# Experts' first layer: from seven products on two-by-two chunks to fifteen on three-by-three-by-two chunks

## The chip, the cores and the metric

The kernel runs on one core of one Trainium2 chip. The metric is the device time of one launch in microseconds (us), the median of several runs. The engines are named as in the profile: PE (TensorE, matrix products, with PEld for its loading of weights), DVE (VectorE), ACT (ScalarE), POOL (GpSimd) and SP (SyncE, which issues most DMAs). Products accumulate in PSUM, in banks of 512 float32 columns; everything else lives in SBUF.

## The reference, cut to what matters

Two layers run over 4 x 1024 tokens of 384 channels. Layer 0 is a deformable attention, layer 1 a linear attention followed by a mixture of experts. The change touches only the experts:

```python
probs = softmax(t @ gate_w + gate_b)              # 4 experts, the best 2 of each token are kept
h = gelu(einsum('bsd,edh->ebsh', t, w1) + b1)     # first layer: 384 -> 1536 units, float32
y = einsum('ebsh,ehd->ebsd', h, w2) + b2          # second layer: 1536 -> 384
out = einsum('bse,ebsd->bsd', masked_probs, y)
```

## The kernel before, in words

The experts run after everything else has nearly ended, from about 1626 us of the span on. The tokens of each expert are cut into 25 blocks: 13 of 512 tokens, 3 of 256 and 9 of 128 (`PHASES`, L40). `ORDER` (L43) fixes their sequence. Written by sizes, with S for 128, it is 512, 512, 512, S, 512, S, 256, 512, S, 512, S, 256, 512, S, 512, S, 256, 512, S, 512, S, 512, S, 512, 512. So six blocks of 512 follow an S, three follow a 256, three follow a 512, and each 256 stands between an S and a 512.

A block's 384 inputs are three chunks of 128 (rows of the first layer's weights `w1`), its 1536 units are twelve chunks of 128. A block of 512 or 256 tokens ("long") is computed with half-blocks of m tokens (256 or 128) as columns:

- The first layer takes two unit chunks at a time (class `Pair`, L2568 on). On the first two input chunks it uses a two-by-two-by-two scheme of seven products P1 to P7 of m columns; the third input chunk is multiplied plainly (`plain`, L2589), which is four more half-width products. A pair thus costs eleven products of m columns, and a block six pairs. Each product on float32 is two PE instructions. Partial results are read out of PSUM while their bank goes on accumulating: ACT copies y after P1 and P5 (L2599), after P6 (L2613) and after P7 (L2630), and DVE adds at L2614, L2615 and L2631.
- The sums of weights that the scheme needs are made by POOL (`first_sums_steps`, L2112 on, four operations of 128x384 for each half of the units, L2121 to L2124). Likewise `second_sums` (L2508 on, four operations of 128x1152) for the second layer. The sums of tokens are made by DVE (`token_sums`, L2494 on, L2503 to L2506).
- The second layer (L2660) is seven accumulated products P1 to P7; DVE makes sums of the hidden units (L2653), adds bias (L2548) and results (L2556) to the rows of the output.
- A block of 128 (`short_block`) uses plain products (L2750, L2762) and no sums. It is called S here.

The order on each engine is written by hand (`tc.manual_schedule`): each engine does its instructions in program order. On POOL, a block j puts in its queue at its start the weight sums of its own second half of units (`first_sums(d, 1)`), `second_sums` part 0, the gather of output rows so far (`rows_so_far`, L2535), `second_sums` part 1, and the first half's sums of the next block (`first_sums(nxt, 0)`); in the middle the gather of the block after next (L2071, one indirect DMA for each 128 tokens); at the end the stores of its rows (`store_rows`, L2563). For an S block only the gathers, the stores and `first_sums(nxt, 0)` remain. For the first block both halves' sums are made long before, between 1525 and 1534 us; its own gathers, `second_sums` and the last routing table entries (L2256) stand before its hooks on POOL. Transposes of the next block (`turn`, PE L2489, DVE copy L2492) and its token sums are spread through the second layer.

Dependencies between engines (semaphores) are set by the framework from the tiles that instructions read and write. PSUM pools: `lmm` with four banks, `lph` and `ltr` with two each.

Of the kernel before, what the change touches and what calls it, by code (L numbers as in the profile page):

```python
# [284 lines left out]
def body(  # L285
# [1819 lines left out]
    HALF_V = HC // 4  # L2105
# [6 lines left out]
    def first_sums_steps(d, half):  # L2112

        if short(d):
            return
        w = d["w1"].rearrange("p a (v m j) -> p a v m j", m=2, j=P)[:, :, half * HALF_V : (half + 1) * HALF_V]
        a11, a21, a12, a22 = w[:, 0, :, 0], w[:, 0, :, 1], w[:, 1, :, 0], w[:, 1, :, 1]
        t = wsum.tile([P, 3, HALF_V, P], F32, tag=f"wa{half}", name=f"wa{half}_{d['i']}")
        s1, s2, s4 = (t[:, k] for k in range(3))
        d["A", half] = dict(P1=a11, P2=a12, P3=s4, P4=a22, P5=s1, P6=s2, P7=a21)  # L2120
        yield nc.gpsimd.tensor_tensor(s1, a21, a22, ALU.add)  # L2121
        yield nc.gpsimd.tensor_tensor(s2, s1, a11, ALU.subtract)  # L2122
        yield nc.gpsimd.tensor_tensor(s4, a12, s2, ALU.subtract)  # L2123
        yield nc.gpsimd.tensor_tensor(a21, a11, a21, ALU.subtract)  # L2124
# [4 lines left out]
    with tc.tile_pool(name="c_1", bufs=1) as c1, tc.tile_pool(name="c_2", bufs=2) as c2, tc.tile_pool(  # L2129
# [255 lines left out]
        def outputs(b):  # L2385
# [42 lines left out]
            if b == 2:  # L2428
                d = state["block"]
                gather(d, ds0, state["added"])  # L2430
                sums = (i_ for half in range(2) for i_ in first_sums_steps(d, half))
            yield
            for k in range(NB):
# [12 lines left out]
                i_ = next(sums, None)  # L2446
                if i_ is not None:
# [26 lines left out]
    with tc.tile_pool(name="d_w1", bufs=1) as dw1, tc.tile_pool(name="d_s1", bufs=1) as ds1, tc.tile_pool(  # L2474
        name="d_2", bufs=2
    ) as d2p, tc.tile_pool(name="d_h", bufs=1) as dh:
        homes = [(dw0, ds0), (dw1, ds1)]
        ds = {0: first}
# [15 lines left out]
        def token_sums(d):  # L2494
# [5 lines left out]
            b11, b12, b21, b22 = x[:, 0, :m], x[:, 0, m:n], x[:, 1, :m], x[:, 1, m:n]  # L2500
            t = d2p.tile([P, 3, 256], F32, tag="xc", name=f"xc{d['i']}")
            t1, t2, t4 = (t[:, k, :m] for k in range(3))
            nc.vector.tensor_tensor(t1, b12, b11, ALU.subtract)  # L2503
            nc.vector.tensor_tensor(t2, b22, t1, ALU.subtract)
            nc.vector.tensor_tensor(t4, b21, t2, ALU.subtract)
            nc.vector.tensor_tensor(b12, b22, b12, ALU.subtract)  # L2506
            d["B"] = dict(P1=b11, P2=b21, P3=b22, P4=t4, P5=t1, P6=t2, P7=b12)
# [66 lines left out]
        class Pair:  # L2574

            def __init__(self, d, v):
                self.d, self.v, self.m = d, v, d["size"] // 2
# [304 lines left out]
```

## Time and profile before

| what | us |
|---|---|
| median of three runs (2637.04 to 2641.66) | 2637.63 |
| the profiled execution's own time | 2639.53 |
| its span, first to last instruction | 2637.8 |
| PE / POOL / DVE / ACT busy in the span | 2476.7 / 1376.8 / 1810.1 / 1102.1 |
| experts: first product to last instruction | 1626.1 to 2637.8 |
| a 512 block after an S: first layer (2188.83 to 2220.92) | 32.09 |
| the same block: second layer (2220.92 to 2245.31) | 24.39 |
| the S block after it (2245.31 to 2261.75) | 16.44 |
| the 256 block after that: first layer, second layer | 18.70, 16.29 |

Reading: "busy" is the union of an engine's instructions, a time after "idle before" is the wait before an instruction and after the arrow stands what ended it. A float32 product appears as "x2" in the timeline, its two passes.

### The profile page before, as it was taken

What the parts mean: (1) busy time and instruction counts of PE and PEld (TensorE: products, weight loads), DVE (VectorE), ACT (ScalarE), POOL (GpSimd) and SP (SyncE); (2) the same over time, 40 slices, a digit from 0 to 9 for tenths busy, and PEclk for the clock granted to TensorE, in tenths of its full rate; (3) what the DMA queues carried; (4) which work ended last, traced back from release to release, by engine and by line L of the source; (5) the groups of instructions that cost most, each with busy time, mean ns of one, the idle gap of its engine ahead of it and who ended that gap; (6) DMA issues with size and microseconds to landing.
All of it is one profiled execution on the core that took longest, in us unless ns stands there. A gap on an engine that the chain in (4) does not pass through costs nothing. (4 is left out here: it accounts for less than half of the span.)

```text
span 2637.8 us, 39381 instructions
## 1 busy us (share of the span) xinstructions
PE 2476.7 (94%) x15017; PEld 1573.9 (60%) x15017; DVE 1810.1 (69%) x2921; ACT 1102.1 (42%) x1818; POOL 1376.8 (52%) x1132
## 2 busy tenths in 40 slices
PE   8989958889999999999999997999999999999999
PEld 5555423333333333333466654888888898888888
DVE  3888959989999999999766667444453444443443
ACT  5666525556666665665433322222222222222222
POOL 1468855765666566566113346444354544734443
PEclk9999979999999999999999998999999999999999
DMA  7774465565556555554312113435545534644431
GB/s 214 199 223 131 146 197 161 151 175 151 156 165 192 175 169 163 158 153 128 120 36 72 65 61 109 150 114 180 186 150 183 192 123 171 234 162 160 151 132 36
DMA packets 263320, 395.42 MB, mean 150 GB/s; under 512 B 134674, under 2 KB 207634, under 8 KB 262748
## 3 DMA queue, kind: packets, MB, share of 16 engines
q1 hardware_dynamic: 214912, 230.43, 28.2%
q0 software_dynamic: 47504, 162.42, 19.5%
q8 instruction: 118, 1.93, 0.3%
q14 instruction: 70, 0.57, 0.1%
q10 hardware_dynamic: 716, 0.07, 0.0%
HBM read 335.95 MB, written 70.06 MB: 154 GB/s over the span
## 5 line engine op out<-in xcount | busy, mean ns | idle before, releaser
L1443 PE MATMUL ps<-q,k 64*64 64x512 f32 (+1 forms) x1632 | 380.4, 583 | 39.9 <-DMA k<-k_d 18.4
L1448 PE MATMUL ps<-t,o 64*64 64x512 f32 (+3 forms) x1536 | 351.8, 572 | 0.0
L1324 POOL DMA_INDIRECT win<-table,widx x192 | 286.6, 1493 | 71.0 <-issue 24.9
L2563 POOL DMA_INDIRECT out<-rows,ei x67 | 67.3, 1004 | 410.9 <-DVE rows L2556 389.8
L1015 POOL DMA_INDIRECT ga<-img,pidx x168 | 205.8, 1225 | 137.9 <-DVE w L972 64.2
L1385 ACT ACTIVATE t<-win,bw 128x1056 f32<-128x1056 f32 x192 | 207.4, 1093 | 128.5 <-DVE S L1475 100.2
L1475 DVE SCALAR_TENSOR_TENSOR S<-t,bw,ps 128x1024 f32<-128x1024 f32 x192 | 237.1, 1277 | 33.8 <-PE ps L1448 31.2
L1443 PEld LDWEIGHTS ps<-q,k 64*64 64x64 f32 x1632 | 104.0, 134 | 259.7 <-issue 193.1
L1548 POOL TENSOR_TENSOR S<-S,pbs 128x896 f32<-128x896 f32 (+1 forms) x69 | 136.8, 1982 | 180.2 <-DVE t L1396 174.7
L1553 ACT ACTIVATE S<-S 128x2048 f32<-128x2048 f32 x96 | 183.4, 1911 | 97.7 <-DVE S L1540 97.7
L1567 PE MATMUL po<-S,v 128*64 128x512 f32 x768 | 193.4, 615 | 24.5 <-ACT S L1553 24.1
L1396 DVE SCALAR_TENSOR_TENSOR t<-win,bw,t 128x1056 f32<-128x1056 f32 (+3 forms) x169 | 196.2, 1196 | 14.4 <-ACT t L1385 11.3
L2660 PE MATMUL b<-w,h 128*128 128x192 f32 x1044 | 180.3, 326 | 0.0
L2660 PEld LDWEIGHTS b<-w,h 128*128 128x128 f32 x1044 | 171.3, 190 | 2.4
L1540 DVE TENSOR_TENSOR S<-S,pbs 128x2048 f32<-128x2048 f32 (+1 forms) x96 | 158.8, 1656 | 13.3 <-ACT pbs L1529 13.3
L2492 DVE COPY d_xT<-e_tr 128x512 f32<-128x512 f32 (+2 forms) x75 | 37.6, 511 | 172.4 <-PE e_tr L2489 172.4
L2599 ACT COPY snap<-y 128x256 f32<-128x256 f32 (+1 forms) x96 | 33.9, 353 | 267.8 <-PE y L2582 267.1
L2256 POOL DMA_INDIRECT tab_d<-ent,si x64 | 65.7, 1027 | 146.8 <-DVE selw L2249 126.9
L2756 ACT ACTIVATE h<-ph,b1c 128x128 f32<-128x128 f32 x108 | 30.9, 369 | 265.0 <-PE ph L2750 265.0
L2614 DVE TENSOR_TENSOR snap<-y,snap 128x256 f32<-128x256 f32 (+1 forms) x96 | 38.4, 400 | 147.6 <-ACT snap L2613 147.5
L2660 PE MATMUL b<-wb,hs 128*128 128x192 f32 x696 | 119.3, 329 | 7.5 <-DVE rows L2556 7.5
L2631 DVE TENSOR_TENSOR y<-y,third 128x256 f32<-128x256 f32 (+1 forms) x96 | 39.1, 407 | 123.0 <-ACT third L2630 123.0
(413 smaller groups left out, 5767.6 us busy)
## 6 DMA issues: line engine op xcount, KB each, us to landing
w<-in_L_ffn_w SPq DMA_DIRECT2D x50, 2304.0 KB
img<-in_x SPq DMA_DIRECT2D x48, 256.0 KB
q<-q_d SPq DMA_DIRECT2D x48, 256.0 KB
x<-in_x SPq DMA_DIRECT2D x8, 768.0 KB
q_d<-qt SPq DMA_DIRECT2D x24, 256.0 KB
v_d<-qkvw SPq DMA_DIRECT2D x32, 192.0 KB
k<-k_d SPq DMA_DIRECT2D x48, 128.0 KB
v<-v_d SPq DMA_DIRECT2D x24, 256.0 KB
```

Source lines behind the costliest of these rows:

```text
L1015: nc.gpsimd.indirect_dma_start(out=ga[:, g].rearrange("p s c -> p (s c)"), out_offset=None, in_=img[b][:, :], in_offset=bass.IndirectOffse ...
L1324: i_ = nc.gpsimd.indirect_dma_start(out=win[:, : (WROWS - free_rows(nb)) * WIN], out_offset=None, in_=tables[h // 2][:, :], in_offset=bass ...
L1385: i_ = nc.scalar.activation(t.rearrange("p y x -> p (y x)"), wins[p, e][:, :n], AF.Copy, scale=weight(p, e, 0),)
L1396: state["gate"] = nc.vector.scalar_tensor_tensor(tf, wins.pop((p, e))[:, WIN : WIN + ts[p, e].shape[1] * WIN], weight(p, e, 1), tf, ALU.mu ...
L1443: made.append(nc.tensor.matmul(ps[HALF[1 - r], e, q_at], k[HALF[r], 2 * kp + e, :], q[HALF[r], q_at], start=(step == 0), stop=(step == 1 a ...
L1448: made.append(nc.tensor.matmul(ps[HALF[r], d, at], os_[p, d][HALF[r], :], wholes[p, d][HALF[r], at.start // WI : at.stop // WI, 0:WI], sta ...
L1475: nc.vector.scalar_tensor_tensor(st[:, e, :].rearrange("p (y x) -> p y x", x=WI), wholes.pop((p, e))[:, :, 1:WIN], weight(p, e, 3), ps[:, ...
L1540: state["gate"] = nc.vector.tensor_tensor(at_, at_, bc(pbss[p // KP][:, cols_], 1, 2), ALU.add)
L1548: i_ = nc.gpsimd.tensor_tensor(at_, at_, bc(pbss[p // KP][:, c_:], 1, 2), ALU.add)
L1553: nc.scalar.activation(Ss[p], Ss[p], AF.Exp)
L1567: nc.tensor.matmul(pos[i][0][HALF[f], :], vs[i][:, 2 * kp + e, :], Ss[p][:, e, FULL[f]], start=(first and e == 0), stop=(last and e == 1),)
L2660: nc.tensor.matmul(out[:, k * NH : (k + 1) * NH], h[:, v, k * P : (k + 1) * P], w[:, v, :], start=(start and v == 0 and k == 0), stop=True ...
```

## The change

The first layer of long blocks now takes three unit chunks, all three input chunks and two token halves at a time, with a scheme of fifteen products q1 to q15 (class `Trio` in place of `Pair`), four trios to a block: 60 products of m columns where there were 66. Nothing of the second layer's arithmetic changes. Two accumulations run in turn, `alpha` (six products in the right half of bank x, for the trio ahead) and `beta` (five products in the right half of bank y); their running contents are tapped, by ACT copies in alpha and by DVE adds in beta, before the next product is added. `two` and `three` put one product each in the left halves of y and x; `shared` and `one` use a bank z of their own. The weight sums become 13 POOL operations of 128x256 for each half of the units, in place of 4 of 128x384. The token sums become 12 DVE operations and one ACT operation, in two parts. For the first block, only the first half's weight sums are still made early; the second half's are now in its `start` hook. The alpha of a block's first trio (`begin`) is issued before the block begins: between the second layer's P3 products of a long block, or the last quarter of an S block's second layer. Transposes of the next block move earlier. The core of the diff, added lines with their places:

```diff
@@ first_sums_steps
-        yield nc.gpsimd.tensor_tensor(s1, a21, a22, ALU.add)
...
+        t = (state["halves"] if half else wsum).tile([P, 6, GH, P], F32, tag=f"wa{half}", name=f"wa{half}_{d['i']}")
+        n0, n1, n2, n3, n4, n5 = (t[:, k] for k in range(6))
+        d["A", half] = dict(
+            q1=a31, q2=a11, q3=n5, q4=n2, q5=a12, q6=n3, q7=n4, q8=a13, q9=n1, q10=n0, q11=a21, q12=a23, q13=a22,
+            q14=a32, q15=a33,
+        )
+        for out_, one, other, op in (
+            (n0, a21, a33, ALU.add), (a31, a31, a32, ALU.add), (n1, a21, a31, ALU.add), (a31, a11, a31, ALU.add),
+            (n2, a32, a31, ALU.subtract), (n2, n2, a33, ALU.subtract), (n3, a13, a23, ALU.subtract),
+            (n4, a21, n3, ALU.subtract), (n3, n3, a22, ALU.add), (n5, a31, a12, ALU.add), (n5, n5, n3, ALU.subtract),
+            (a23, a23, a33, ALU.add), (a23, a23, a22, ALU.subtract),
+        ):
+            yield nc.gpsimd.tensor_tensor(out_, one, other, op)
@@ token_sums(d, part)
+            if part == 0:
+                nc.scalar.mul(x9, b11, -1.0)
+            for out_, one, other, op in (
+                (
+                    (x0_, b12, b11, ALU.subtract), (b12, b12, b22, ALU.subtract), (x1, b12, b32, ALU.subtract),
+                    (x2, b11, x1, ALU.subtract), (x3, b11, b22, ALU.subtract),
+                ),
+                (
+                    (x6, b32, b31, ALU.subtract), (x7, x6, b12, ALU.subtract), (x5, b21, b31, ALU.add),
+                    (x4, b21, b22, ALU.subtract), (b21, b11, b21, ALU.subtract), (x8, b22, b31, ALU.add),
+                    (b32, b22, b32, ALU.add),
+                ),
+            )[part]:
+                nc.vector.tensor_tensor(out_, one, other, op)
@@ class Trio
+            def alpha(self, k):
...
+                self.product(("q10", "q11", "q9", "q1", "q2", "q4")[k], self.x, self.right, start=k == 0)
+                if k < 5:
...
+                    nc.scalar.copy(to, self.x[:, self.right])
+            def beta(self, k):
...
+                self.product(("q15", "q12", "q6", "q8", "q7")[k], self.y, self.right, start=k == 0)
+                if k < 4:
...
+                    nc.vector.tensor_tensor(to, self.y[:, self.right], to, ALU.add)
+                else:
+                    nc.vector.tensor_tensor(self.y[:, self.both], self.y[:, self.both], self.th[:, self.both], ALU.add)
+            def shared(self):
+                self.z = lph.tile([P, 512], F32, tag="ph", name="z")
+                self.product("q3", self.z, self.left, start=True)
...
+            def one(self):
+                self.product("q5", self.z, self.left)
...
+            def two(self):
+                self.product("q13", self.y, self.left)
+            def three(self):
+                self.product("q14", self.x, self.left)
...
@@ long_block, first layer
+                order = (
+                    "a0 t q b0 a1 r b1 a2 s b2 a3 u p b3 a4 b4 v a5" if ahead else
+                    "f t q f b0 f r f b1 f s f b2 f u p f b3 f f b4 v"
+                ).split()
+                # a, b: alpha of the trio ahead, beta; q shared, r two, s three, p one;
+                # t, u, v: gelu of the trio before's second, this one's third and first unit chunk;
+                # f: a step of the second layer's P1
@@ long_block, second layer
             if nxt:
-                turn(nxt, 1)
+                turn(nxt, 2)
+                token_sums(nxt, 0)
             add_rows(d, high, 1, b3_)
             second_product(d, "P7", b1_, range(HV), False)
...
+            third, more = second_steps(d, "P3", b3_, range(HV), False), begin(nxt)
+            for _ in third:
+                next(third, None)
+                next(more, None)
+            for _ in more:
+                pass
             add_rows(d, high, 1, b1_)
             add_rows(d, high, 0, b1_)
             store_rows(d, high)
+            if nxt:
+                token_sums(nxt, 1)
             add_rows(d, low, 1, b3_)
@@ short_block, behind first_layer(2)
+                turn(nxt, 2)
+                token_sums(nxt, 0)
+            second_layer(0)
+            second_layer(1)
             add_bias(d, 0)
-            second_layer(2)
+            if nxt:
+                token_sums(nxt, 1)
+            second_layer(2, True)
+            for _ in more:
+                pass
@@ before the blocks
+            for part in range(2):
+                token_sums(first, part)
+            for _ in begin(first):
+                pass
@@ hooks("start")
                         if j == 0:
+                            first_sums(d, 1)
                             first_sums(nxt, 0)
```

In the written order a and b are alpha of the trio ahead and beta; q is `shared`, r `two`, s `three`, p `one`; t, u, v are the gelu of the trio before's second and of this trio's third and first unit chunk (ACT); f is a step of the second layer's P1 (one product of 192 columns, two PE instructions). In the second layer of a long block `turn(nxt, 0)` now stands behind P4, `turn(nxt, 1)` behind P6 and `turn(nxt, 2)` behind P5; in an S block `turn` of parts 0 and 1 stands before the last third of its first layer. `begin(d)` issues the six alphas of trio 0; `second_layer(2, True)` issues one of them before each of its four products.

## The prediction, as it was put on record

> **What bounds the kernel now.** I read the page's busy times, then the experts' stretch alone: the windows of single stages, the timeline of one pair, POOL's timeline, and the waits. PE is busy 94% of the span, and in the experts' 512 blocks all of the time. The windows (length; busy us of PE, PEld, DVE, ACT, POOL; clock) of a 512 block's first and second layer, the S behind it, and a 256 block's two layers:
>
> ```profile
> 2188.83:2220.92 32.09, 31.94 (x141) 25.92 (x140) 10.54 (x20) 14.15 (x29) 21.25 (x16) 1.00 0.41 132
> 2220.92:2245.31 24.39, 24.39 (x153) 24.32 (x151) 14.39 (x25) 0.69 (x1) 1.85 (x2) 1.00 0.30 106
> 2245.31:2261.75 16.44, 16.44 (x104) 13.16 (x103) 5.03 (x9) 3.43 (x12) 8.34 (x10) 1.00 0.97 330
> 2261.75:2280.45 18.70, 18.37 (x132) 15.77 (x130) 7.38 (x20) 9.53 (x29) 17.06 (x13) 1.00 0.68 228
> 2280.45:2296.74 16.29, 13.74 (x88) 13.27 (x87) 15.22 (x20) 0.47 (x1) 10.76 (x8) 1.00 0.43 159
> ```
>
> Here PE sets the end, except in the 256 block, where POOL works 17 of 18.7 us. Now the timeline inside a pair:
>
> ```profile
> 2199.56 1.02 PE L2589 MATMUL x<-d_xT,w 128*128 128x512 f32 x2
> ...
> 2203.88 0.59 PE L2582 MATMUL y<-xc,wa 128*128 128x256 f32 x2
> ...
> 2204.31 1.02 PE L2589 MATMUL x<-d_xT,w 128*128 128x512 f32 x2
> 2204.56 0.37 ACT L2599 COPY snap<-y 128x256 f32<-128x256 f32 x1 [0.49 <-PE y L2582]
> ...
> 2204.99 0.37 PEld L2582 LDWEIGHTS y<-xc,wa 128*128 128x128 f32 x2 [0.49 <-ACT snap L2599]
> 2205.16 0.59 PE L2582 MATMUL y<-xc,wa 128*128 128x256 f32 x2
> ```
>
> A pair lasts 2204.31 - 2199.56 = 4.75 us for eleven half-width products: 0.431 each, with no wait left on PE. And the tap has a length: product 0.59, then 0.09, copy 0.37, 0.05 to the weights, 0.18 to the next product in the same bank, 1.28 from start to start; it is hidden because three products' time (1.29) lies between. With DVE as the reader: 0.59, some 0.03, 0.43 (L2614), 0.15 from its end to the product (below), 1.20. **I take 1.25 for both.**
>
> ```profile
> 1897.39 0.28 DVE L2614 TENSOR_TENSOR snap<-y,snap 128x128 f32<-128x128 f32 x1
> ...
> 1897.82 0.46 PE L2582 MATMUL y<-d_xT,w 128*128 128x128 f32 x2 [0.59 <-DVE snap L2614]
> ```
>
> This product is P7: it writes the left half of y, and it waits for a DVE add that reads the right half. A bank is guarded as a whole.
>
> POOL, around an S and the 256 block behind it (S from 1878.45, the block from 1894.89), and when POOL is first free in the first block:
>
> ```profile
> 1889.35 0.99 POOL L2535 DMA_INDIRECT rows<-out,ei  x1 [7.74 <-DMA out<-rows,ei]
> 1890.35 1.02 POOL L2121 TENSOR_TENSOR wa<-w 128x384 f32<-128x384 f32 x1
> ...
> 1900.38 1.02 POOL L2563 DMA_INDIRECT out<-rows,ei  x1 [0.30 <-issue]
> 1901.41 1.02 POOL L2121 TENSOR_TENSOR wa<-w 128x384 f32<-128x384 f32 x1
> ...
> 1905.49 2.62 POOL L2522 TENSOR_TENSOR wb<-w 128x1152 f32<-128x1152 f32 x1
> ```
>
> ```profile
> 1648.82 0.96 POOL L2256 DMA_INDIRECT tab_d<-ent,si  x1 [0.30 <-issue]
> 1649.79 1.01 POOL L2121 TENSOR_TENSOR wa<-w 128x384 f32<-128x384 f32 x1
> ```
>
> **What the change saves.** Six products of m columns a block: 6 x 0.431 = 2.59 us in 13 blocks and 6 x 0.227 = 1.36 in three, 37.7 us, if PE never waits.
>
> **512 blocks, first layer.** A trio is 15 products, 6.47. By the written order the products of one chain are three slots apart (1.29, hidden), but for two places. `two` (r) stands two slots behind b0, whose DVE add reads the same bank: 1.25 - 0.86 = 0.39. b4 stands two behind b3: 0.39. (a5 behind a4 is widened by b4's wait.) 7.25 a trio. ACT (5 copies, 3 gelus of 0.69: 3.9) and DVE (7 x 0.43 + 0.70 = 3.7) have room. The last trio: 9 products, ten P1 steps of 0.325 (24 instructions in 3.90), waits of 0.49 (b0, f, r) and 0.17 (b3, f, f, b4): 7.79. Three and one: 29.5, where 32.09 stood for the same work: -2.55, in the 12 blocks after the first **-30.6**.
>
> [...]
>
> **The alphas ahead (`begin`).** Behind a 512: between P3 steps a chain link is 0.65 + 0.43 = 1.08, short of 1.25 by 0.17, five times; with 6 x 0.431 that is 3.4, three times: **+10.3**. In an S before a 512: 2.59, four links short by 0.13 (0.69 + 0.43), one by 0.82: 3.9, six times: **+23.6**. On DVE the S's bias add (L2548) waits for the gathered rows until 16.6 to 18.3 us after the S began; behind it now stand seven token sums and the S's row add. Alone a token sum takes 0.42, beside POOL's sums it took 0.8 to 1.1; at 0.8 they last to about 23, the block's first DVE taps come some 1.3 late, r waits for them: 6 x 1.3 = **+7.8**.
>
> **POOL.** 128x256 is not in the trace: 384 columns take 1.00, 1152 take 2.62, by that line 256 take 0.73, with 0.07 pause 0.80; 13 take 10.4 in place of 4.2. Ends: 0.70 (in proportion) and 1.09 (no saving by size). I take the line, whose points are the same operation. 512 blocks cover it: behind a 512 the second half's sums start 3 us into the block, and trio 2's alpha wants the first of them at 7.2; behind an S with one gather, some 4 in.
>
> First block: the second half's sums, once made at 1530, now start at 1649.8, behind the table entries. Trio 2's alpha, due about 1647, waits for 1650.6; shared wants the 11th (1658.6), b1 the 13th (1660.2), 5.7 more end that trio at 1666, the last 7.8 at 1674, where the second layer began at 1665.6: **+8.4**.
>
> 256 blocks: POOL's sums in the S run 1890.35 to 1900.75, cast and four gathers 5.9, the store 1.0; the second half's first sum is there at 1908.5, the 11th at 1916.5, the 13th at 1918.1. A link here is 0.39 + 0.06 + 0.28 + 0.2 = 0.93. Trio 2's alpha would start by 1904: it starts at 1908.6, its trio waits again at 1916.5 and 1918.1, ends 3.5 later, the last takes 5.4: 1927, for 1915.3 now. Of these 11.7 us 2.1 are `begin` (6 x 0.227, a link of 0.70): three times **+6.3** and, at 9.5, **+28.5**. Behind it P3 has only six steps: alphas last 0.65 + 5 x 1.25 + 0.43 = 7.3, P3 covers 1.95, +5.4; POOL's next sums, now to about 1940, lie beside DVE's hidden and token sums and hold the first alpha some 2: 7.3, three times **+22**.
>
> SP's transfers and the earlier transposes I cost at nothing: weights have a whole block, and the transposes' number is unchanged; if PE's cover went, 0.15 each.
>
> **Sum**: -30.6 + 10.3 + 23.6 + 7.8 + 8.4 + 6.3 + 28.5 + 22 = +76 on the profiled execution's 2639.5 (span 2637.8 and 1.7 around it): 2716. The median lies 1.9 lower: **2714**.
>
> **The clock.** Behind a wait of 2.40 us before 2104.35 the granted clock was 0.58 from 2105 to 2109; behind two like it, no loss: up to 1.7 us each, some nine such waits, 0 to 15 in the range. [...]
>
> **Rivals.**
> 1. POOL is in time: sums fit beside what PE does. For it: one PE wait on POOL over 1 us now. Against: its 17 of 18.7 us. Then 256 blocks pay only their links (-8 and -2 each), the first block some 1.5: 76 - 30 - 7 = 39, 2677.
> 2. Not slower: the taps cost nothing, because a link is no longer than two slots. Then a 512's first layer is 54 x 0.431 + 3.25 = 26.5, -67 in twelve; begins cost 9 x 2.6 + 3 x 1.4 = 28, the first block 5, the 256 blocks 21 and 8: -5, 2633. It decides at a link of 0.86; each 0.1 above costs about 20. Against: the 1.28 of ACT's row.
> 3. POOL's 128x256 costs as 128x384: 3.8 more a half; 256 blocks +11 each, 512 behind S +4 each, first block +3: 60 more, 2774.
>
> **Numbers.** Forecast 0.60 (2690 to 2740), rival 1 0.17, rival 2 0.13 (0.09 faster, 0.04 same), rival 3 0.10. The range 2655 to 2765 takes in the first two, the clock, POOL's lower end, and half of rival 3. A difference of 0.2% is about what a measurement of this kernel can tell from none. Faster 0.09, same 0.04, slower 0.87.
>
> **What would show it.** Right: a steady trio of 7.2 us with two PE waits of 0.4 ended by DVE; a 512's first layer 29 to 30; PE waits on POOL's weight sums in the 256 blocks and near 1650; alphas 1.2 apart. Wrong: trios of 6.5, or POOL operations of 0.6 or 1.0, or a 256 block not longer than 40 us.

## The result and the profile after

The kernel after the change takes 2716.38 us (median of four runs, 2710.62 to 2722.44), the kernel before 2637.82 on the same chip (four runs): 1.0294 times the time, 95% interval 1.0281 to 1.0308. The change makes the kernel slower by about 79 us. The forecast was 2714.

The profiled execution of after has a span of 2714.6 us, 76.8 more than before's; PE is busy 2496.5 us, 20 more though it multiplies less, and POOL 1572.9, 196 more.

Blocks are named by their place in `PHASES`: 0 to 12 have 512 tokens, 13 to 15 have 256, 16 to 24 are S; block 11 is the last 512 behind an S. First the windows of single stages of the kernel after (length; busy us of PE, PEld, DVE, ACT, POOL with their instructions; granted clock; DMA share; GB/s): the first layer of a 512 block behind a 512, the first and the second layer of a 512 block behind an S, the S behind it, and the first and second layer of the 256 block behind that (block 15).

```profile
1756.76:1786.03 29.27, 28.57 (x129) 23.07 (x128) 14.20 (x33) 12.31 (x26) 26.59 (x25) 1.00 0.40 129
2237.78:2269.13 31.35, 28.75 (x130) 22.99 (x129) 17.00 (x36) 12.42 (x26) 28.62 (x29) 1.00 0.35 119
2269.13:2293.51 24.38, 24.38 (x152) 24.32 (x151) 15.09 (x26) 0.85 (x2) 3.42 (x4) 1.00 0.34 122
2293.51:2312.00 18.49, 18.04 (x116) 14.40 (x115) 4.75 (x12) 4.95 (x18) 9.95 (x13) 1.00 0.89 310
2312.00:2340.82 28.82, 21.72 (x121) 18.68 (x119) 13.13 (x39) 8.37 (x26) 25.99 (x28) 0.82 0.42 137
2340.82:2364.84 24.02, 17.67 (x101) 15.27 (x99) 19.50 (x30) 2.92 (x8) 21.90 (x22) 1.00 0.43 145
```

The 512 block did get shorter (29.27 where 32.1 stood, 31.35 behind an S). The S got longer by 2.05, and the 256 block by 10.1 and 7.7 us. In the 256 block PE is busy 21.72 of 28.82 us and POOL 25.99: there the bound has passed from PE to POOL; the granted clock is 0.82 there, of which more below. The second layer of a 512 block that stands before an S is unchanged (24.38); before another 512 it takes 28.5 to 29.4 where 25.4 stood, with the next block's alphas in it.

Now PE's timeline inside a steady trio (start and length; the first and the last row are the first products of this trio and of the next):

```profile
1763.94 0.59 PE L2605 MATMUL x<-xc,wa 128*128 128x256 f32 x2
...
1764.80 0.59 PE L2605 MATMUL y<-xc,w 128*128 128x256 f32 x2
1765.23 0.60 PE L2605 MATMUL x<-xc,w 128*128 128x256 f32 x2
1765.91 0.70 PE L2605 MATMUL y<-xc,w 128*128 128x256 f32 x2
1766.45 0.59 PE L2605 MATMUL y<-d_xT,w 128*128 128x256 f32 x2
...
1771.12 0.59 PE L2605 MATMUL x<-xc,wa 128*128 128x256 f32 x2
```

and what DVE does meanwhile:

```profile
1765.43 0.42 DVE L2632 TENSOR_TENSOR tc<-y,tc 128x256 f32<-128x256 f32 x1
```

The product at 1764.80 is b0, the one at 1765.23 is a1, the one at 1765.91 is r. b0 and r stand two slots apart, 0.86 us if nothing waits, and start 1.11 apart, because DVE's read of b0's result begins at 1765.43. The next product then starts 0.54 behind r, not 0.43. So one such wait costs 0.25 + 0.11 = 0.36. A trio has two, at r and at b4, and lasts 1771.12 - 1763.94 = 7.18 where fifteen products alone take 6.47.

The waits of the experts' stretch, summed (total, times, longest), for these two places:

```profile
PEld y L2605 <- DVE tc L2632: 45.6, 63, 2.7
PEld y L2605 <- DVE tg L2632: 26.7, 68, 0.6
```

The first line is mostly r, long where DVE is late behind an S; the second is mostly b4.

The 256 block behind an S, first POOL's timeline (the last gather of the middle, the store, the first of the second half's sums, the eleventh):

```profile
2319.27 0.94 POOL L2072 DMA_INDIRECT xr<-tn_d,ei  x1 [0.30 <-issue]
2320.51 1.02 POOL L2586 DMA_INDIRECT out<-rows,ei  x1 [0.30 <-DVE tg L2645]
2321.55 0.75 POOL L2133 TENSOR_TENSOR wa<-w 128x256 f32<-128x256 f32 x1
...
2329.25 0.72 POOL L2133 TENSOR_TENSOR wa<-wa 128x256 f32<-128x256 f32 x1
```

and the waits in PE's timeline of the same block, first layer and second layer (the last row is the first alpha of the next block):

```profile
2316.53 0.79 PE L2605 MATMUL y<-xc,w 128*128 128x128 f32 x2 [2.21 <-DVE tc L2632]
2322.35 0.49 PE L2605 MATMUL x<-xc,wa 128*128 128x128 f32 x2 [0.43 <-POOL wa L2133]
...
2330.02 0.49 PE L2605 MATMUL z<-d_xT,wa 128*128 128x128 f32 x2 [2.49 <-POOL wa L2133]
...
2357.66 0.92 PE L2694 MATMUL b<-w,hs 128*128 128x192 f32 x4 [3.19 <-DVE rows L2579]
2358.41 0.60 PE L2605 MATMUL x<-xc,wa 128*128 128x256 f32 x2
```

Trio 2's alpha starts at 2322.35, 0.05 behind the end of POOL's first sum of that half; the shared product of trio 2 starts at 2330.02, 0.05 behind the end of the eleventh. These two rows set the length of the first layer up to 2330.02: time lost before them, as the 2.21 us at 2316.53, costs nothing. What is lost behind the second row counts. A part of that is the clock: from 2332.08 to 2335.49 it was 0.5. The stretch from the shared product of trio 2 to the second layer, here and in the 256 block at the same place of e2 (below; its first layers have the same products, sums and order), where the clock was 1.00:

```profile
2330.02:2340.82 10.80, 9.99 (x57) 8.80 (x57) 4.44 (x15) 3.14 (x9) 10.17 (x7) 0.84 0.12 36
2416.13:2425.91 9.78, 8.82 (x57) 7.43 (x58) 4.43 (x15) 3.52 (x10) 9.15 (x7) 1.00 0.08 22
```

This stretch is 9.78 us in all three 256 blocks of e2 (clock 1.00 in the one shown); in after it is 11.63, 10.73 and 10.80, with 5.9, 3.4 and 3.4 us at half clock. So half clock costs 3.8 us in the three. The second layer waits for row adds of DVE, 1.34, 0.25 and 3.19 us, and then the six alphas take from 2358.41 to 2364.84.

The first block, PE's alphas and POOL's timeline (the first two sums stand ahead of the table entries, the other eleven behind them):

```profile
1628.99 1.19 PE L2605 MATMUL x<-xc,wa 128*128 128x256 f32 x2 [7.24 <-issue]
1630.69 1.22 PE L2605 MATMUL x<-xc,w 128*128 128x256 f32 x2 [0.51 <-ACT th L2622]
```

```profile
1623.70 0.73 POOL L2133 TENSOR_TENSOR wa<-w 128x256 f32<-128x256 f32 x1
1624.40 0.71 POOL L2133 TENSOR_TENSOR w<-w 128x256 f32<-128x256 f32 x1
...
1648.82 0.74 POOL L2133 TENSOR_TENSOR wa<-w 128x256 f32<-128x256 f32 x1
1649.63 0.73 POOL L2133 TENSOR_TENSOR w<-w 128x256 f32<-128x256 f32 x1
```

Six alphas with nothing to lie beside, at a granted clock of 0.50, 1.68 apart: the first product of block 0 itself starts at 1638.43, where it was 1626.13 before.

### The profile page after: what moved, and what is told of

Same layout as the page of the kernel before. It is cut to its first block, busy times and chain, and to the rows that moved or that the text cites. A ratio compares the mean times of both kernels' runs of the same rounds, so it can differ in the third digit from the quotient of the medians.

```text
span 2714.6 us, 40034 instructions
## 1 busy us (share of the span) xinstructions
PE 2496.5 (92%) x15017; PEld 1579.1 (58%) x15017; DVE 1948.0 (72%) x3273; ACT 1111.0 (41%) x1866; POOL 1572.9 (58%) x1420
## 4 chain that ended last, share of the span: by engine, by line
PE 47%; DVE 23%; issue 11%; POOL 10%; DMA 6%; ACT 3%; SPq 0%; DVEq 0%; POOLq 0%; ACTq 0%
PE b L2694 7%; PE ps L1444 6%; DVE S L1476 4%; PE x L2605 4%; PE y L2605 4%; PE po L1568 4%; PE c_kv L2368 4%; POOL ga L1016 3%; DVE m L1494 3%; DVE S L1541 2%; PE c_y L2445 2%; PE po L1577 2%; DVE t L1397 2%; POOL wa L2133 2%; ACT S L1554 1%
## 5 line engine op out<-in xcount | busy, mean ns | idle before, releaser
L1325 POOL DMA_INDIRECT win<-table,widx x192 | 284.7, 1483 | 70.3 <-issue 25.4
L1568 PE MATMUL po<-S,v 128*64 128x512 f32 x768 | 194.4, 618 | 24.0 <-ACT S L1554 23.5
L2694 PE MATMUL b<-w,h 128*128 128x192 f32 x1044 | 196.8, 327 | 0.8 <-DVE rows L2579 0.8
L2605 PE MATMUL y<-xc,w 128*128 128x256 f32 (+1 forms) x384 | 117.9, 390 | 24.7 <-DVE tc L2632 20.9
L2814 ACT ACTIVATE h<-ph,b1c 128x128 f32<-128x128 f32 x108 | 30.8, 368 | 265.0 <-PE ph L2808 265.0
L2579 DVE SCALAR_TENSOR_TENSOR rows<-b,en,rows 128x192 f32<-128x192 f32 x232 | 85.0, 410 | 68.5 <-PE b L2694 68.2
L2622 ACT COPY th<-x 128x256 f32<-128x256 f32 (+1 forms) x128 | 45.1, 352 | 217.4 <-PE x L2605 217.4
L2133 POOL TENSOR_TENSOR wa<-w 128x256 f32<-128x256 f32 x160 | 129.0, 806 | 5.3
```

Source lines behind the costliest of these rows:

```text
L1325: i_ = nc.gpsimd.indirect_dma_start(out=win[:, : (WROWS - free_rows(nb)) * WIN], out_offset=None, in_=tables[h // 2][:, :], in_offset=bass ...
L1568: nc.tensor.matmul(pos[i][0][HALF[f], :], vs[i][:, 2 * kp + e, :], Ss[p][:, e, FULL[f]], start=(first and e == 0), stop=(last and e == 1),)
L2605: nc.tensor.matmul(out[:, at], d["A", self.g // GH][what][:, self.g % GH], d["B"][what], start=start, stop=True, skip_group_check=True,)
L2694: nc.tensor.matmul(out[:, k * NH : (k + 1) * NH], h[:, v, k * P : (k + 1) * P], w[:, v, :], start=(start and v == 0 and k == 0), stop=True ...
```

## The experiments

My theory: the saved products are outweighed by chain links (a product, its read-out, the next product in that bank) which PE can't cover, and in the 256 blocks by POOL's thirteen sums for each half. The main rivals: the 512 blocks lose by something else than the guarded bank; the 256 blocks lose by links alone. The kernels e1 to e8 ran on chips where the kernel before takes 2729 to 2731 us, since the stages ahead of the experts end some 80 us later there (the first transposes of the experts start at 1685 to 1701 us, not at 1615); e9, e10 and e11 ran where it takes 2636 to 2638. Ratios are always to the kernel before on the same chip. They can't be set off against each other across chips to better than about 0.3% (one kernel, e8 and e11, has 0.9916 on one and 0.994 on the other), so single effects are read from the lengths of blocks in the traces, most of which repeat to 0.1 us where the clock is full, and sums of them from the time between block 0's second layer and the last product: 965.9 us in before, 1037.8 in after. In the tables "first" runs from a block's own first product (behind the alphas ahead) to its second layer, "second" from there to the next block's first product.

### e1: `two` ahead of the chain, in the bank before the chain starts

```diff
-                    "a0 t q b0 a1 r b1 a2 s b2 a3 u p b3 a4 b4 v a5" if ahead else
+                    "a0 t r b0 a1 q b1 a2 s b2 a3 u p b3 a4 b4 v a5" if ahead else
-                    "f t q f b0 f r f b1 f s f b2 f u p f b3 f f b4 v"
+                    "f t r f b0 f q f b1 f s f b2 f u p f b3 f f b4 v"
@@ beta(k)
-                self.product(("q15", "q12", "q6", "q8", "q7")[k], self.y, self.right, start=k == 0)
+                self.product(("q15", "q12", "q6", "q8", "q7")[k], self.y, self.right)
@@ two()
-                self.product("q13", self.y, self.left)
+                self.y = lmm.tile([P, 512], F32, tag="mm", name="y")
+                self.product("q13", self.y, self.left, start=True)
```

> The changed kernel with one thing moved: the product of `two` (left half of bank y) is issued before b0 instead of two slots behind it, so no tap of that bank stands before it; `shared` takes its slot. Theory A (the bank is held until the DVE tap has read it, a DVE link is 1.11 us from product to product in the trace after): r loses 0.25 us in three trios and 0.35 in the last, 1.1 us in each of 13 blocks of 512: 2716 - 14 = 2702 us, steady trio 6.95 instead of 7.2 us. With the 1.25 of the prediction it would be 21.6 less, 2695. Theory B (PE waits there because DVE is late with its queue, not because of the bank): the wait moves to b1 and the time stays within 3 us of 2716.

Measured: 2784.73 us, ratio 1.0190 (1.0168 to 1.0211). The windows of the same two 512 blocks, behind a 512 and behind an S:

```profile
1844.62:1872.49 27.87, 27.61 (x129) 23.07 (x128) 14.30 (x33) 12.32 (x26) 25.44 (x23) 1.00 0.42 135
2320.31:2349.34 29.03, 27.79 (x129) 23.07 (x128) 16.54 (x36) 12.41 (x26) 26.57 (x26) 1.00 0.38 128
```

27.87 for 29.27: -1.41, four times 0.35, one wait in each trio. Behind an S the mean falls from 31.90 to 29.55. So the bank guarded as a whole is what r waits for; nothing of the arithmetic or of DVE's work was changed. The guard is a semaphore that the framework sets; no run here shows what would happen without it. The wait at b4 is still there. From block 0's second layer to the last product e1 takes 1020.8 us, 17 less than after (expected 14).

### e2: the S's bias add behind the token sums

```diff
-            add_bias(d, 0)
             if nxt:
                 token_sums(nxt, 1)
+            add_bias(d, 0)
```

> The changed kernel with the S block's bias add (DVE, waits for the gathered rows and for b2's load) placed behind the second part of the next block's token sums instead of ahead of it. Theory A (the 2.6 us that a 512 block behind an S needs more than one behind a long block are the queue of seven token sums behind that bias add): its first layer falls from 31.9 (mean of six) to 29.3, six times, -16, and up to 1 us in each 256 block: 2716 - 16 = 2700, not below 2697. Theory B (these blocks wait for POOL's weight sums, made in the S): no change, 2716.

Measured: 2798.34 us, ratio 1.0247 (1.0220 to 1.0274). Five of the six 512 blocks behind an S are within 0.9 us of the others (29.28, 29.40, 30.18, 29.39, 30.16; block 11 is at 31.26; mean 29.95 for 31.90), and the wait at r in the block at 2122.51 is down to:

```profile
2124.61 0.70 PE L2605 MATMUL y<-xc,w 128*128 128x256 f32 x2 [0.21 <-DVE tc L2632]
```

where after had 1.81 to 2.31 in such blocks. In after, ahead of the block at 2237.78, these are the bias add on DVE and then r on PE:

```profile
2234.40 0.65 DVE L2571 SCALAR_TENSOR_TENSOR rows<-b2r,en,rows 128x384 f32<-128x384 f32 x1 [4.24 <-DMA rows<-out,ei]
2241.82 0.70 PE L2605 MATMUL y<-xc,w 128*128 128x256 f32 x2 [1.98 <-DVE tc L2632]
```

So most of what a 512 block loses behind an S is the row's DMA: the bias add waits for the gathered rows, and token sums and taps stand behind it in DVE's queue.

### e3: the 256 blocks without weight sums

The kernel leaves out POOL's weight sums in the 256 blocks: their products read plain weights, so these results are not those of the reference.

```diff
@@ first_sums_steps
+        if d["size"] == 256:
+            d["A", half] = {f"q{k + 1}": w[:, k % CK, :, k // CK % 3] for k in range(15)}
+            return
```

> The changed kernel without POOL's weight sums of the first layer in the three blocks of 256 tokens: the products read plain weights in place of sums, so these blocks' results are not those of the reference. [...] Theory B (the length of these blocks is the chain of taps at 0.87 us a link and the half clock behind the waits): at most 2 us a block, 2710 or more.

Measured: 2765.61 us, ratio 1.0123 (1.0104 to 1.0143). The windows of the same 256 block, first and second layer:

```profile
2377.12:2397.41 20.29, 17.95 (x120) 15.07 (x119) 11.07 (x39) 8.39 (x26) 17.09 (x13) 1.00 0.50 169
2397.41:2417.91 20.50, 17.41 (x101) 15.24 (x100) 14.97 (x30) 2.92 (x8) 13.69 (x15) 1.00 0.52 174
```

The three first layers are 21.93, 20.08 and 20.29 (29.60, 28.48, 28.82 with the sums), the second layers 20.6, 20.5, 20.5 (23.2, 25.7, 24.0). POOL's 26 sums cost some 8.2 us in the first layer and 3.8 in the second, for which links are no explanation, as the links are the same here. In the first layer about 1.3 of the 8.2 is the half clock of after behind its waits on POOL (the 3.8 us of three blocks above); in the windows of e3 shown here the clock is 1.00. What is left above before (18.7 to 20.4 and 16.3 to 17.7) was not taken apart further; links and alphas are left to explain it.

### e4: the first block's second sums made earlier

```diff
-        read, sums, written = rows_so_far(first), second_sums(first, 0) + second_sums(first, 1), last_entries()
-        made += sums[:1] + read[:2] + sums[1:2] + read[2:] + sums[2:3] + written[:4] + sums[3:] + written[4:]
+        read, sums = rows_so_far(first), second_sums(first, 0) + second_sums(first, 1)
+        mine, written = list(first_sums_steps(first, 1)), last_entries()
+        made += sums[:1] + read[:2] + sums[1:2] + read[2:] + sums[2:3] + mine + written[:4] + sums[3:] + written[4:]
```

> The changed kernel with the first block's second half of weight sums placed on POOL before the last routing table entries instead of behind them. Theory A (prediction: the first block waits for these sums, 8 us, of which the two taps behind a slow start are 1): 2716 - 6 = 2710. Theory B (the trace after: PE waits for no sum there; the 4.8 us come from the six alphas that go one by one at half clock before the block begins): within 2 us of 2716; the table entries, 10 us later, may hold the next block's gather but not PE.

Measured: 2819.94 us, ratio 1.0318 (1.0280 to 1.0355). No gain: the first block's first layer is 40.65 us, where e1, e2 and e3, which leave these sums where they were, have 38.86, 39.33 and 38.90 on that chip; and the first alpha comes 18.06 us behind the first transpose in place of 14.23. The 8.4 us that the prediction put down to these sums are not there to be had: in the trace of after PE's one wait for them in block 0 is 0.2 us. Neither expectation (6 us less, or no change) holds, as the start of the experts got some 5 us longer; why was not looked into. The 512 blocks behind block 0 are as in after: 29.28 but for one (30.47), and behind an S 30.4 to 31.2 but for two (33.57 and 32.92).

### e5: every link three slots or more

e1 and e2 together, and the order rewritten: the last alpha of a trio (e) moves to the trio's own start, `two` of the next trio (n) between a4 and b4, so that b4 stands three slots behind b3; `begin` issues five alphas.

```diff
-                    "a0 t q b0 a1 r b1 a2 s b2 a3 u p b3 a4 b4 v a5" if ahead else
-                    "f t q f b0 f r f b1 f s f b2 f u p f b3 f f b4 v"
+                    "a0 t r e b0 a1 q b1 a2 s b2 a3 u p b3 a4 n b4 v" if g == 0 else
+                    "a0 t e b0 a1 q b1 a2 s b2 a3 u p b3 a4 n b4 v" if ahead else
+                    "e f t b0 f q f b1 f s f b2 f u p f b3 f f f b4 v"
```

> The changed kernel with an order in which every tap has at least three products' time: `two` of a trio is issued ahead of its beta, the sixth alpha product behind the first alpha product of the next trio, b4 three slots behind b3; and the S block's bias add behind the token sums. Theory A (the taps, not the number of products, keep a 512 block's first layer at 29.3 us): it falls to 55 products of 0.431 and ten P1 steps, 27.0 us with the sixth alpha inside it, in blocks behind an S too (31.9); the S before a 512 falls from 20.9 to about 19.6. Sum about -59 us, ratio to the kernel before 1.007. Theory B (DVE and ACT, with 3.7 and 3.9 us a trio and their queues, set the pace): the first layer stays over 28 us, ratio above 1.015.

Measured: 2764.64 us, ratio 1.0130 (1.0103 to 1.0158), less gain than expected. A 512's first layer is 27.49 behind a 512 (expected 27.0) and 27.8 to 28.1 behind an S, but for block 11 (30.26; why that one stays longer was not looked into, here and in the kernels below); an S before a 512 is 19.66 for 20.89. The 256 blocks are not helped: 29.1, 29.0, 27.9 and 23.5, 25.8, 26.8. From block 0's second layer to the last product e5 takes 998.9 us, 39 less than after (expected 59). Of the miss some 11 us lie in the 512 first layers (0.5 in each, 0.4 more behind an S, block 11); the 256 blocks, with their second layers, are 2 us longer than in after.

### e6, e7, e8: plain first layers in the 256 blocks

The fifteen-product order of e5, the kernel after, and the kernel before, each with the first layer of the three 256 blocks computed plainly, 36 products of 256 columns, no weight sums and no token sums for them:

```diff
+            if lesser(d):
+                for u in range(HC):
+                    ps = lmm.tile([P, 512], F32, tag="mm", name="x")
+                    for c in range(CK):
+                        nc.tensor.matmul(
+                            ps[:, : 2 * m], d["w1"][:, c, u * P : (u + 1) * P], d["xT"][:, c, : 2 * m],
+                            start=(c == 0), stop=(c == CK - 1),
+                        )
```

> The kernel e5_order with the three blocks of 256 tokens computed plainly: 36 products of 256 columns in the first layer, no weight sums, no token sums, no alphas for them. Theory A (these blocks lose by POOL's sums): their first layer is 36 x 0.431 + 5 P1 steps = 17.2 us where it was 29, second layer with the next block's alphas about 19.5 where it was 24.3, the S before them 16.4: -56 us, ratio 0.986, below the kernel before. Theory B (the rest of a 256 block's length is DVE's token sums and the chain of alphas of the next 512): second layer stays above 23, ratio 0.992.

> The changed kernel with only the three blocks of 256 tokens computed plainly (36 products of 256 columns, no sums). Theory A (of the loss of 77 us some 57 are in and around these three blocks): 17.6 us less for each, -53, ratio 1.010; 512 blocks unchanged at 29.3 and 31.9. Theory B (the loss is the 512 blocks' taps and alphas): ratio above 1.02.

> The kernel before with the three blocks of 256 tokens computed plainly, as a control for e6 and e7. Theory A: first layer 17.2 us for 18.7 to 20.4, second layer 16.3 and without the waits on DVE that stood beside POOL's sums: -8 us, ratio 0.997. Theory B (the seven-product scheme still pays at 128 columns): ratio 1.000 or above.

| | us | ratio (interval) | 256 first | 256 second |
|---|---|---|---|---|
| e7, after with plain 256 | 2754.23 | 1.0083 (1.0054 to 1.0113) | 17.16 | 23.4, 22.1, 23.6 |
| e6, e5 with plain 256 | 2712.87 | 0.9936 (0.9916 to 0.9955) | 17.16 | 22.4, 22.3, 20.3 |
| e8, before with plain 256 | 2706.09 | 0.9916 (0.9887 to 0.9946) | 17.2 to 17.4 | 13.3 to 14.0 |

e7 answers to what was expected in the total: with the 256 blocks out of the scheme 1.0083 is left of 1.0294. Part of that is not the change's doing, as e8 shows. Its 512 blocks behind an S take 30.8 (mean of six; expected 31.9). e6 gained less than expected, since its second layers stayed at 20 to 22 and not 19.5. e8 gained more than expected, and shows why a control is worth a run: before's own seven-product scheme, with its sums, did not pay in these blocks (17.2 for 18.7 to 20.4, and 13.3 for 16.3 to 17.7; by these lengths 16.5 us, less than the ratio on this chip says). With it e6's gain over before is no proof for the fifteen products: e6 and e8 can't be told apart. The 4.6 us that e6 wins in each first layer of a 512 (27.49 for 32.10) go back in the alphas ahead and in 8 us behind each 256.

### e9: tokens prepared earlier

e6 with the next block's transposes and all its token sums in the middle of a 256's first layer, or behind the first third of an S's first layer:

```diff
@@ long_block, plain first layer
+                    if u == 6:
+                        for c in range(CK):
+                            turn(nxt, c)
+                        token_sums(nxt, 0)
+                        token_sums(nxt, 1)
@@ short_block
             first_layer(0)
+            for c in range(CK):
+                turn(nxt, c)
+            token_sums(nxt, 0)
+            token_sums(nxt, 1)
             first_layer(1)
```

> The plain-256 version of the new order, with what prepares the next block moved ahead. In a 256 block the next block's transposes and both parts of its token sums stand after six unit chunks of the plain first layer, and the five alphas are spread over the first two second-layer steps; in an S block the transposes and both parts of the token sums stand after the first third of its first layer, and the alphas at second-layer steps 4, 6, 8, 10 and 11 instead of 8 to 11. Theory A, the handover that a 256 block gives back (second layer and alphas 20.3 to 22.4 us against 13.34 in the kernel before with plain 256 blocks) is the chain of late token sums and alphas: 256 second layer and alphas about 15.5 (three times -6.5, -20 us), S to 512 from 19.66 to about 19.3, 512 behind an S from 28.0 to 27.5; together about -25 us, ratio to the kernel before about 0.985, under the 0.992 of the kernel before with plain 256 blocks. Theory B, it is GpSimd's weight sums for the next block that come late, whatever the token sums do: 256 second layer and alphas stay above 20, ratio not under 0.991.

Measured: 2635.07 us, ratio 0.9986 (0.9977 to 0.9995). Behind an S it worked: every 512 there takes 27.49, as behind a 512, but block 11 (28.95). Behind the 256 theory A failed: its second layer still takes 22.1 to 23.2, and its first layer grew from 17.16 to 19.04. In all e9 lost by the move: from block 0's second layer to the last product it takes 957.8 us, e6 951.0. But B, POOL's sums for the next block, is not what holds it either. DVE's timeline of the kernel e9 in a 256 block, POOL's, and the wait on PE:

```profile
2085.37 6.09 DVE L2533 TENSOR_TENSOR xc<-d_xT 128x256 f32<-128x256 f32 x1
2091.49 0.83 DVE L2533 TENSOR_TENSOR d_xT<-d_xT 128x256 f32<-128x256 f32 x1
```

```profile
2085.89 2.64 POOL L2552 TENSOR_TENSOR wb<-w,wb 128x1152 f32<-128x1152 f32 x1
2088.47 2.63 POOL L2553 TENSOR_TENSOR w<-w 128x1152 f32<-128x1152 f32 x1
2091.05 0.98 POOL L2136 TENSOR_TENSOR wa<-w 128x256 f32<-128x256 f32 x1
```

```profile
2092.33 4.06 PE L2696 MATMUL b<-w,h 128*128 128x192 f32 x24
...
2104.14 5.55 PE L2696 MATMUL b<-wb,hs 128*128 128x192 f32 x24 [5.80 <-DVE rows L2582]
```

One token sum lasts 6.09 us, until two of POOL's 128x1152 operations are over; the others, beside POOL's 128x256 sums, take 0.83 and more. DVE comes to the sums of hidden units (`hs`) at 2100.89 only, the row adds stand behind those, and PE waits 5.80 for a row add to free its bank. The granted clock of this layer is 0.92 (about 3.5 of its 22.07 us at a half), and the 24 instructions as this wait ends take 5.55 where 24 took 4.06 before it; so 1.5 of the 22 us is the clock. The first alpha follows at 2110.18, and POOL's sums had ended at 2102.94. So a third theory, C: DVE's one queue, slowed by POOL, holds the second layer of a 256, whether the token sums stand late (e6) or early (e9).

### e10 and e11: the 256 blocks plain in both layers, and the control beside it

To test C the 256 blocks lose the second layer's scheme too: twelve products of 384 columns for each of two token tiles, no sums on POOL, no `hs` on DVE, the next block's alphas between the second tile's products.

```diff
@@ second_sums
-            if short(d):
+            if short(d) or lesser(d):
@@ long_block, behind the plain first layer
+                token_sums(nxt, 0)
+                token_sums(nxt, 1)
...
+                more = begin(nxt)
+                for s_ in range(2):
+                    acc = lph.tile([P, 512], F32, tag="ph", name="acc")
+                    for hc in range(HC):
+                        nc.tensor.matmul(
+                            acc[:, :NC], h[:, hc, s_ * P : (s_ + 1) * P], d["w2"][:, hc, :],
+                            start=(hc == 0), stop=(hc == HC - 1),
+                        )
+                        if s_ and hc % 2:
+                            next(more, None)
```

> The 256 blocks are computed plainly in both layers: 36 products of 256 columns, then two token tiles of twelve products of 384 columns, so they need no weight sums of the first or second layer and no sums of hidden units; the next block's transposes stand at the middle of their first layer, its token sums behind it, its alphas between the second tile's products. S blocks before a 512 as in the early-token version, S blocks before a 256 with their transposes before the last third. Theory C, the 256 block's handover is DVE: its token sums and sums of hidden units stand in one queue, each beside GpSimd sums that slow it, and products wait for the row adds behind them. Then 256 second layer and alphas are 24 x 0.65 + 5 x 0.43 = 17.7, where 20.3 to 23.2 stood with either place of the token sums, and first layer 17.2 to 18.5; experts from block 0's second layer to the end about 946, ratio about 0.992. Theory B, GpSimd's sums for the next 512 block hold its first alpha: no gain under 20 for the second layer, ratio not under 0.997.

> The control on the same chip: the kernel before with plain first layers in the 256 blocks. By the block lengths of the earlier look (first layer 17.2, second layer 13.3 to 14.0) 16.6 us under the kernel before, ratio 0.9937. Theory 'the fifteen products pay when the 256 blocks are out of their way': the plain-both kernel is under this one by about 10 us. Theory 'the two schemes are even here': within 0.2 per cent of each other.

Measured on one chip: e10 2613.37 us, ratio 0.9915 (0.9901 to 0.9929); e11 2620.50, ratio 0.9940 (0.9926 to 0.9953). Windows of e10: a 512's first layer behind an S, a 256's first and second layer:

```profile
2178.05:2205.54 27.49, 27.49 (x131) 23.84 (x130) 14.50 (x32) 12.51 (x26) 25.05 (x26) 1.00 0.42 137
2246.88:2264.48 17.60, 17.25 (x85) 14.91 (x84) 9.96 (x13) 5.22 (x11) 9.96 (x13) 1.00 0.70 236
2264.48:2282.12 17.64, 17.64 (x59) 11.02 (x58) 6.32 (x8) 2.64 (x7) 7.10 (x9) 1.00 0.44 157
```

The second layer with the alphas takes 17.64 in all three blocks (expected 17.7), PE busy in all of it, though it multiplies more than e6 did: as C expects, no wait is left. By itself e10 does not part C from B, since it frees POOL as well as DVE; that POOL's sums for the next block were not waited for is shown by the trace of e9. All of e10's windows above run at a granted clock of 1.00. e10 is the fastest kernel of the study, 23 us under before and 7 under the control (expected 10); the two intervals touch. From block 0's second layer to the last product the control takes 948.4 us and e10 937.2. The control has the better start: from the first transpose to block 0's second layer 49.3 us, e10 54.1.

## Why the prediction was right, by its steps

The profiled span grew by 76.8 us; the prediction's terms add up to 76. The mechanisms were right in the main, but that the sum came out to 1 us is luck: three terms missed, by -3.2, +7.9 and -3.6 us, and nearly cancel; two had a cause that was wrong in part; and the measured terms hold some 7 us of half clock that the prediction kept out of its sum. Term by term (before and after from the two traces):

| term | predicted | measured |
|---|---|---|
| 512 first layers, the twelve after the first | -30.6 | 12 x (29.28 - 32.10) = -33.8 |
| the same behind an S, DVE's queue | +7.8 | 6 x (31.90 - 29.28) = +15.7 |
| alphas ahead in an S before a 512 | +23.6 | 6 x (20.89 - 17.10) = +22.7 |
| alphas ahead behind a 512 | +10.3 | 3.17 + 3.17 + 4.02 = +10.4 |
| alphas ahead in an S before a 256 | +6.3 | 3 x 2.05 = +6.2 |
| 256 first layers | +28.5 | 9.2 + 9.0 + 10.1 = +28.3 |
| 256 second layers | +22 | 6.9 + 8.0 + 7.7 = +22.6 |
| first block, end of its first layer | +8.4 | 1670.39 - 1665.55 = +4.8 |

- **The link.** It was taken as 1.25 for both engines. ACT's is 1.15 to 1.24 (alphas in an S, where they stand in the last third of its second layer), DVE's 1.11, and behind a waited link 0.11 more is lost. So each of the two waits in a trio costs 0.36, not 0.39; the steady trio is 7.18 (predicted 7.25), and a 512 first layer without DVE's delay 29.28 (predicted 29.5). e1 takes one of the waits away alone and gets the 0.35 per trio.
- **The bank guard.** Right: r waits for a read of the bank's other half, and is free once it stands ahead of the chain; e1 finds 1.41 us a block in it, 18 in thirteen, and more behind an S.
- **DVE's queue behind an S.** The mechanism was right (e2 takes it away), the size was half: 7.8 predicted, 15.7 measured. The term that was mis-sized is the 1.3 us a block by which the taps come late: it is 2.05, or 12.3 in six blocks. The other 3.4 us are the clock: in two of the six blocks (33.35 and 32.92 us, the others 31.0 to 31.5) it fell to half for 3.4 us right behind r. Ahead of the block at 2237.78 (S from 2216.90) the bias add ends at 2235.05; the seven token sums, 0.83 to 0.95 each but the last, end at 23.7 us, the row add at 24.2, and r, which waits 1.98, starts at 2241.82.
- **POOL's sums.** The line through 384 and 1152 columns gave 0.73 for 128x256 and 0.80 from start to start; the trace has 0.72 to 0.75 alone, and 0.69 to 0.81 from start to start (beside DVE's sums of hidden units, 1.7 to 2.3 each, one takes up to 2.3). Rival 3 (as dear as 384 columns) and POOL's end of 1.09 are out. In the 256 blocks trio 2's alpha and shared product start 0.05 behind the sums that were named; e3 takes the sums away and 8.2 us go. That 28.3 stands for 28.5 is in part chance: 3.8 of it is half clock behind the second of these rows. Rival 1 (POOL is in time) is out by this; rival 2 (links no longer than 0.86) by the 1.11 and 1.2.
- **The 256 second layer.** 7.3 was predicted, 5.4 of it for alphas past P3 and 2 for POOL holding the first one. The size is right, the holder of the 2 only half: before waited 2.4 to 2.55 us for row adds in that layer, after waits 4.78 in block 15 (1.34, 0.25 and 3.19; 3.96 and 4.87 in the other two), and POOL's sums are not waited for. What POOL does is slow DVE's queue: four of the five token sums ahead of the last row add take 0.83 to 0.94 beside POOL's sums, and 0.41 to 0.43 once these have ended. e9 and e10 put the wait down to DVE as well.
- **The first block.** The step that failed here: trio 2's alpha does not wait for POOL at about 1650. Two of the sums ran in a gap ahead of the table entries, and PE itself was later by then, so the rest were in time. What block 0 loses it loses ahead of its first own product, with six alphas at half clock (0.50) and nothing to put between them, which the prediction had left out here. Earlier sums gain nothing (e4).
- **The clock.** The prediction allowed 0 to 15 us for some nine waits, at up to 1.7 each, and had none in its sum. There were nine stretches of half clock (0.50) behind block 0, six of 3.4 us and three of 6.8: six in the first layers of the 256 blocks (3.8 us lost), two in 512 blocks behind an S (1.7 each), one in a second layer of a 256, where before has one too. What the change adds by them is about 7 us.
- **What the change saves** was read rightly but small: 37.7 us of products in all, of which only the 512 blocks realise some.

## What to carry to other kernels

A scheme with fewer products pays only where its chains find cover: count, for each link, how many other products stand between a product and the next one that needs its bank read, and compare with the measured link (here 1.1 to 1.2 us, three products of 256 columns). Price the extra sums by stage, not on average: the smallest blocks, with few columns to spread the sums of weights over, turned from PE-bound to POOL-bound in their first layers, and these blocks held two thirds of the loss (28.3 in the first layers and 22.6 in the second, of 76.8 us). And run the same repair on the kernel before: plain 256 blocks gave it 0.6 to 0.8% by themselves, so that the fifteen products at their best order and place are worth about 0.3%, hardly more than can be told apart here.

## What the runs showed of the hardware that was not expected

- **DVE beside POOL.** A token sum of 128x256 on DVE takes 0.42 alone, 0.83 to 0.95 beside POOL's 128x256 sums (0.73 alone, 0.79 to 0.98 beside token sums in e9) but for three of 2.10 in after, and 6.09 in e9 beside two of POOL's 128x1152 operations, 2.64 and 2.63. That one ends at 2091.46, 0.36 behind the second of the two. Why it lasted through both, though it had started 0.52 us before the first, no run here shows.
- **Half clock behind short waits.** In after the granted clock falls to a half in the first layers of the 256 blocks, where PE waits for 0.7 to 2.5 us three or four times in each block. Here are windows in block 15, where PE waited from 2314.32 to 2316.53:

```profile
2315.20:2318.60 3.40, 2.07 (x9) 2.07 (x10) 1.57 (x6) 0.27 (x1) 2.52 (x3) 0.50 1.06 385
2318.60:2322.00 3.40, 3.32 (x15) 2.77 (x13) 1.61 (x5) 1.31 (x4) 2.78 (x4) 0.52 1.01 349
```

  In this block POOL's sums would have held trio 2's alpha to 2322.35 in any case. Where no such row comes behind it, the time is lost: in a 512 block behind an S, after a wait of 2.31 us, products start 0.85 apart where 0.43 is usual,

```profile
2038.62 1.06 PE L2605 MATMUL x<-d_xT,w 128*128 128x256 f32 x2
2039.47 1.06 PE L2605 MATMUL y<-xc,wa 128*128 128x256 f32 x2
```

  and from r to the next trio 6.9 us pass where 5.2 pass in such blocks at full clock. No wait in the first layers of the 256 blocks is longer than 2.5 us. In the 3.4 us ahead of each of the nine stretches, as long as the shortest of them, PE was busy for 0.2 to 1.9 us; what exactly decides stays open. The length of one wait alone does not: in after half clock began within a wait of 1.88 us at r in a 256 block, while two waits of 1.98 at r in 512 blocks were followed by a clock of 1.00, as in before two of 2.54 and 2.55 for row adds.
- **A waited link costs more than its wait.** Behind a product that waited, the next one starts 0.54 later, not 0.43, so a wait of 0.25 costs 0.36.
